# Newton steps of two demodulation weights on GpSimd instead of VectorE, and their squares issued one stage earlier on ScalarE

## The chip, the cores and the metric

The kernel runs on one core of a Trainium2 chip. The metric is the device time of one execution in microseconds, as the median of the runs shown; lower is better. The engines are TensorE (PE: matrix multiplies, PEld: its weight loads), VectorE (DVE), ScalarE (ACT), GpSimd (POOL) and SyncE (SP, which issues the DMA transfers). Each engine executes its own stream of instructions in order and waits on semaphores for the results of the others.

## The reference

The program is a stack of four residual layers over an input of 64 sequences, 64 positions and 256 channels: two attention layers conditioned on a style vector, then two state-space (recurrent) layers. The change touches only the first attention layer, so that is what is shown:

```python
def _dcoef(weight, style):
    return rsqrt(einsum('oi,bi->bo', square(weight), square(style)) + 1e-8)

s1, s2 = styles[:, :256], styles[:, 256:]
x = x * s1[:, None, :]
x = (x - mean(x)) * rsqrt(var(x) + 1e-5)            # over channels
q_dc = _dcoef(q_weight, s1); k_dc = _dcoef(k_weight, s1); v_dc = _dcoef(v_weight, s1)
w_dc = _dcoef(w_weight, s2); u_dc = _dcoef(u_weight, s2)
q = heads((x @ q_weight.T) * q_dc)
k = heads((x @ k_weight.T) * k_dc)
v_flat = (x @ v_weight.T) * v_dc * s2
attn = softmax(q @ k.T * scale)
out  = (attn @ heads(v_flat)) @ w_weight.T * w_dc
skip = v_flat @ u_weight.T * u_dc
return out + skip                                   # added to the layer's input
```

The five vectors `q_dc` to `u_dc`, one value per output channel and sequence, are called demodulation coefficients here. They depend on the weights and the styles only, not on `x`.

## The kernel before

**Layout and staging.** Channels lie on the 128 partitions (two halves of 128), tokens along the free dimension. The 4096 tokens are cut into 8 blocks of 512 for attention; with two layers that makes 16 attention blocks (`Att`, numbered 0 to 15), about 32 us each. After them 16 blocks of the state-space layers follow, driven by a recurrence over time steps. All weights and all of `x` stay on chip.

**The order of the work.** Every instruction is pinned to the program order. The attention part writes this order from a list of events: each part of a block has a due time in units of one block's duration, relative to the block's number (`att_plan`: `(-0.836, "style")` means that block n's `style` is issued at n - 0.836). The events are sorted by due time and called in this order, so an earlier due time only means an earlier place in the stream of each engine; no instruction waits for a clock.

**An attention block.** `style` multiplies `x` by the style, `fold1` adds the two channel halves, `mean` multiplies by a matrix of 1/256 on TensorE (tile `pm`), `center` subtracts that on VectorE and squares on ScalarE (tile `sq`), `fold2` adds the halves of the squares, `var` is the second mean (tile `pv`), `root` takes the logarithm and exponential on ScalarE (tile `rs`), `norm` multiplies. `style`, `fold1`, `fold2` and `norm` run on VectorE for block 0 and on GpSimd for all others (`engine()`). Then come the projections (`q`, `k`, `v`; TensorE tile `pw`), `scores` (tile `ps`, four groups per block), the softmax (`soft_a`: maximum `mx`, subtraction and exponential `pr`; `soft_b`: sum and reciprocal `sm`, then scaling on GpSimd), transposes of the probabilities (`turn`, tile `pt`), transposes of the values (`values`, also named `pv` on the page, shape 64x64 or 128x64; `values_out` copies them on ScalarE into `v`), `attend` (tile `po`), and the two output projections `out` with weights 4 (`u`) and 3 (`w`), whose results are multiplied by the coefficients on VectorE (tile `t`). Small matmul results share three rotating PSUM buffers (`aps`), so a matmul may have to wait for whoever reads the buffer three uses earlier.

**The coefficients.** `demodulate` is a generator that is advanced by events, one stage at each call, for the weights in the order 0, 1, 2, 4, 3 (q, k, v, u, w). Each weight has four stages: (1) the square of the weights on ScalarE (tile `wsq`); (2) eight matmul records on TensorE with the squared styles (tile `dca`) and a copy with bias on ScalarE (tile `newton`); (3) logarithm and exponential on ScalarE (tile `dc`), a first value of the reciprocal root; (4) a Newton step that refines it: two multiplies, one multiply-add and one multiply of 128x128 elements. Stage 4 is on VectorE for the first attention layer and on GpSimd for the second. `first` is the generator of the first layer; the second layer's is advanced later, one stage at a time. The coefficients of weight 4 are first read by block 0's `out` at 0.183 and those of weight 3 by its `out` at 1.422.

At 0.05 four stages of `first` are due at once, all of weight 4; at 0.7 four more, all of weight 3. Around them stand, of block 0: `scores` 0 (-0.243), `soft_a` 0 (-0.054), `v` 1 (-0.050), `scores` 1 (0.034), `soft_a` 1 (0.090), `out` 4 (0.183), `values` 0 (0.213), `values_out` 0 (0.259), `values` 1 (0.341); of block 1: `style` (0.164), `fold1` (0.174), `mean` (0.176), `center` (0.181), `fold2` (0.194), `var` (0.370), `root` (0.386), `norm` (0.402), `q`, `k` (0.522 to 0.693), `v` 0 (0.736); of block 2: `style` (1.164), `fold1` (1.174), `mean` (1.176).

Before block 0, `warm` issues matmuls on constants to keep TensorE busy while the first inputs arrive.

Of the kernel before, what the change touches and what calls it, by code (L numbers as in the profile page):

```python
# [41 lines left out]
def bc(ap, axis, n):  # L42

    ap = ap.unsqueeze(axis)
    shape = list(ap.shape)
    shape[axis] = n
    return ap.broadcast_to(shape)
# [13 lines left out]
def tile_kernel(ctx: ExitStack, tc: tile.TileContext, ins, out):  # L61
    nc = tc.nc
# [43 lines left out]
    def mm(*args, **kw):  # L106
        pin(nc.tensor.matmul(*args, **kw))  # L107
# [4 lines left out]
    def act(*args, **kw):  # L112
        pin(nc.scalar.activation(*args, **kw))  # L113
# [474 lines left out]
    with tc.tile_pool(name="xpool", bufs=1) as xpool, tc.tile_pool(  # L588
# [35 lines left out]
        def demodulate(l, pool, tag):  # L624

            dc = dcs[l] = xpool.tile([P, 5, HC, B], FP, tag=f"dc{l}", name=f"dc{l}")

            kd = kds[l] = xpool.tile([P, HC, B, 2], FP, tag=f"kd{l}", name=f"kd{l}")
            for w in (0, 1, 2, 4, 3):
                wsq = pool.tile([P, HC, H], FP, tag=tag, name=f"wsq{l}_{w}")  # L630
                act(wsq, att_w[l][:, w, :, :], AF.Square)
                yield
                p = aps.tile([P, HC, B], FP, tag="w", name=f"dca{l}_{w}")
                for oc in range(HC):
                    for k in range(HC):
                        mm(
                            p[:, oc, :],
                            wsq[:, k, oc * P : (oc + 1) * P],
                            csq[:, (0 if w < 3 else HC) + k, :],
                            start=(k == 0),  # L640
                            stop=(k == HC - 1),
                        )
                d = dc[:, w, :, :]
                e = a1.tile([P, HC, B], FP, tag="newton", name=f"newton{l}_{w}")
                act(e, p, AF.Identity, bias=eps_dm)
                yield
                act(d, e, AF.Ln)
                act(d, d, AF.Exp, scale=-0.5)
                yield

                eng = nc.vector if l == 0 else nc.gpsimd

                def times(o, a, b):
                    pin(eng.tensor_tensor(o, a, b, ALU.mult))

                times(e, e, d)
                times(e, e, d)

                g = float(H // NH) ** -0.5 if w == 1 else 1.0
                pin(eng.tensor_scalar(e, e, -0.5 * g, 1.5 * g, ALU.mult, ALU.add))  # L660
                times(d, d, e)
                if w == 1:
                    times(d, d, dc[:, 0, :, :])
                    times(kd, bc(d, 3, 2), bc(bc(mask_par, 1, B), 1, HC))
                elif w == 2:

                    times(d, d, cT[:, 2:4, :])
                yield
# [253 lines left out]
        functions()  # L922
        warm(20)
        first, second = demodulate(0, a2, "t4"), demodulate(1, a1, "sq")
        plan0 = prepare(0, lambda name: e8.tile([P, TB], FP, tag="xc", name=name))

# [4 lines left out]
        def at(when, *parts):  # L931
            events.extend((when, b, part, args) for b, part, *args in parts)
# [4 lines left out]

        for when, k in (
            (-0.835, 1), (-0.823, 2), (-0.805, 2), (-0.613, 2), (-0.597, 2), (-0.477, 1),
            (-0.345, 2), (0.05, 4), (0.7, 4),  # L940
        ):
            at(when, *[(first, None)] * k)
        at(-0.822, (warm, None, 14))
# [254 lines left out]
```

## Time and profile before

| | |
|---|---|
| median of 3 runs | 1598.27 us (1596.71 to 1598.61) |
| profiled execution, own time | 1596.88 us |
| its span, first to last instruction | 1595.0 us |
| TensorE busy | 1527.8 us (96%) |
| VectorE busy | 1311.3 us (82%) |
| ScalarE busy | 1121.8 us (70%) |
| GpSimd busy | 862.4 us (54%) |
| mean granted TensorE clock | 0.993 |

A row of the profile names an engine, the line of the program, the operation, and output<-inputs by their tile names without numbers; times are in us. "Idle before, releaser" is how long the engine waited just before the instruction, and which instruction ended that wait. The line can be that of a helper: L107 is every matmul, L110 every transpose, L113 every ScalarE activation, L123 most two-input operations of VectorE, L654 the multiplies of the Newton step and L660 its multiply-add; so the tile names tell the instructions apart. An fp32 matmul appears as two records. "PEclk" is the granted TensorE clock, as a share of full speed, in forty equal slices of the span; TensorE's busy times are modelled and include pipelining.

### The profile page before, as it was taken

Reading aid. Unit: us, or ns where it says so; the run is one execution under the profiler, and the core shown is the slowest. Engines: PE = TensorE matmul, PEld = TensorE weight load, DVE = VectorE, ACT = ScalarE, POOL = GpSimd, SP = SyncE. Lnnn points to the kernel's source line nnn. Section 1 sums busy time; section 2 is a strip of 40 time slices with the busy share of each in tenths; the row PEclk is TensorE's granted clock in tenths of the full one; section 3 lists DMA queues with packets and bytes.
Section 4 is the critical chain, followed back from the end, with each engine's and each line's share of the span. In section 5 each row is a group of like instructions: output and inputs, shape, how many; then the busy total and the mean of one; then the engine's idle time right before and its main releaser. Section 6 shows DMA issues by size and latency. Waiting matters only on the chain. (4 is left out here: it accounts for less than half of the span.)

```text
span 1595.0 us, 30321 instructions
## 1 busy us (share of the span) xinstructions
PE 1527.8 (96%) x12440; PEld 669.0 (42%) x12440; DVE 1311.3 (82%) x1483; ACT 1121.8 (70%) x1899; POOL 862.4 (54%) x859
## 2 busy tenths in 40 slices
PE   8999999999999688999999999999999999999888
PEld 5555555555555333333333333333333333333324
DVE  5776767777777688989999999999899899998776
ACT  3555554455456468888878888887888887887774
POOL 1667566556667657365455464654564545635420
PEclk9999999999999799999999999999999999999999
DMA  7000000000000020000000000000000000000001
GB/s 242 2 1 2 2 2 1 2 2 2 1 2 2 1 64 1 1 1 1 1 1 1 1 1 1 1 1 1 1 8 7 14 1 14 15 1 14 7 8 27
DMA packets 19337, 18.26 MB, mean 11 GB/s; under 512 B 5472, under 2 KB 16352, under 8 KB 19200
## 3 DMA queue, kind: packets, MB, share of 16 engines
q1 hardware_dynamic: 19200, 16.34, 3.2%
q8 instruction: 98, 1.61, 0.4%
q14 instruction: 39, 0.32, 0.1%
HBM read 12.14 MB, written 4.19 MB: 10 GB/s over the span
## 5 line engine op out<-in xcount | busy, mean ns | idle before, releaser
L113 ACT ACTIVATE v<-h,ad 128x512 f32<-128x512 f32 x1008 | 649.0, 711 | 111.2 <-DVE h L1099 109.4
L1099 DVE CUSTOM_DVE_ANT_0 h<-v,pu 128x1024 f32<-128x1024 f32 x504 | 593.7, 1217 | 98.6 <-ACT v L113 50.9
L107 PE MATMUL pu<-xn,bd 32*128 32x512 f32 x2048 | 292.8, 640 | 34.2 <-DVE h L1099 29.8
L107 PE MATMUL py<-h,cd 128*32 128x512 f32 x2048 | 246.3, 598 | 0.0
L206 POOL TENSOR_TENSOR xr<-xr,cT 128x512 f32<-128x512 f32 x55 | 70.5, 1282 | 311.7 <-ACT xr L205 311.6
L107 PE MATMUL pw<-xm,aw 128*128 128x512 f32 x384 | 178.0, 602 | 0.0
L107 PEld LDWEIGHTS pu<-xn,bd 32*128 32x128 f32 x2048 | 82.3, 183 | 172.0 <-issue 99.7
L825 POOL TENSOR_TENSOR pr<-pr,sm 128x1024 f32<-128x1024 f32 x64 | 121.1, 1903 | 21.7 <-DVE sm L824 20.2
L107 PE MATMUL pg<-xt,win 128*128 128x512 f32 x256 | 127.0, 618 | 0.0
L107 PE MATMUL pw<-z,wo 128*128 128x512 f32 x240 | 125.6, 625 | 0.0
L117 DVE SCALAR_TENSOR_TENSOR acc<-xr,cv,acc 128x512 f32<-128x512 f32 x165 | 123.7, 750 | 1.6 <-ACT acc L113 0.2
L107 PE MATMUL acc<-xt,win 128*128 128x512 f32 x256 | 124.3, 609 | 0.7 <-ACT xc L113 0.7
L107 PEld LDWEIGHTS py<-h,cd 128*32 128x32 f32 x2048 | 53.5, 109 | 164.1 <-issue 163.8
L839 ACT COPY pT<-pt 128x512 f32<-128x512 f32 x128 | 68.4, 586 | 76.5 <-PE pt L110 76.5
L113 ACT ACTIVATE pr<-pr 128x1024 f32<-128x1024 f32 x64 | 67.7, 1057 | 60.7 <-DVE pr L123 60.7
L107 PEld LDWEIGHTS pw<-xm,aw 128*128 128x128 f32 x384 | 68.5, 190 | 68.0 <-issue 64.5
L440 POOL TENSOR_TENSOR dx<-xn,rep 128x512 f32<-128x512 f32 x64 | 81.2, 1279 | 18.7 <-DVE ys L123 18.7
L814 DVE TENSOR_REDUCE mx<-ps 128x16 f32<-128x1024 f32 x64 | 78.3, 1224 | 13.7 <-PE ps L107 13.7
L323 POOL TENSOR_TENSOR xn<-xg,rep 128x512 f32<-128x512 f32 x64 | 82.0, 1280 | 8.0 <-ACT xg L113 3.3
L721 POOL TENSOR_TENSOR sq<-sq 128x512 f32<-128x512 f32 x15 | 19.2, 1277 | 122.8 <-ACT sq L113 122.8
L123 DVE TENSOR_TENSOR pr<-ps,mx 128x1024 f32<-128x1024 f32 x64 | 78.4, 1225 | 8.2
L123 DVE TENSOR_TENSOR t<-pw,dc 128x512 f32<-128x512 f32 x64 | 44.2, 690 | 44.9 <-PE pw L107 43.7
(155 smaller groups left out, 2315.0 us busy)
## 6 DMA issues: line engine op xcount, KB each, us to landing
xt<-in_xT SPq DMA_DIRECT2D x8, 512.0 KB, 8.5
out_xT<-xt SPq DMA_DIRECT2D x14, 256.0 KB, 2.3
aw<-in_aw SPq DMA_DIRECT2D x10, 256.0 KB, 6.6
win<-in_win SPq DMA_DIRECT2D x2, 1024.0 KB, 9.0
rep<-in_rep SPq DMA_DIRECT2D x2, 784.0 KB, 7.2
wo<-in_wo SPq DMA_DIRECT2D x2, 512.0 KB, 8.6
out_xT<-xt SPq DMA_DIRECT2D x2, 192.0 KB, 2.5
wx<-in_wx SPq DMA_DIRECT2D x2, 96.0 KB, 7.9
```

What stands on the lines that cost most here:

```text
L107: pin(nc.tensor.matmul(*args, **kw))
L113: pin(nc.scalar.activation(*args, **kw))
L117: nc.vector.scalar_tensor_tensor(out=out, in0=in0, scalar=scalar, in1=in1, op0=op0, op1=op1)
L123: pin(nc.vector.tensor_tensor(*args))
L206: pin(nc.gpsimd.tensor_tensor(curb, curb, bc(temb, 2, BT), ALU.add))
L323: pin(nc.gpsimd.tensor_tensor(self.xn[j], xg, self.rep[:, DI : 2 * DI], ALU.add))
L440: pin(nc.gpsimd.tensor_tensor(self.dx[j], self.xn[j], self.rep[:, 2 * DI : 3 * DI], ALU.mult))
L721: pin(self.engine().tensor_tensor(a, a, self.sq[:, 1, :], ALU.add))
L814: pin(nc.vector.tensor_reduce(mx, s4, AX.X, ALU.max))
L825: pin(nc.gpsimd.tensor_tensor(pr, pr, bc(sm, 3, S), ALU.mult))
L839: pin(nc.scalar.copy(self.pT[g][:, c, :, :], pt))
L1099: nc.vector._custom_dve(TENSOR_ADD_SAT, out=hn, in0=vs.pop((i, h)), in1=pu[h], s0=10.0, s1=-10.0)
```

## The change

The Newton step of weights 4 and 3 of the first attention layer goes from VectorE to GpSimd; for weights 0, 1 and 2 it stays on VectorE. In the event list, one of the four stages due at 0.05 (the square of weight 4) is now due at -0.1, and one of the four due at 0.7 (the square of weight 3) at 0.3. The other three stages of each weight keep their due times.

```diff
@@ in demodulate, stage 4
-                eng = nc.vector if l == 0 else nc.gpsimd
+                eng = nc.vector if l == 0 and w < 3 else nc.gpsimd
@@ the events of the first layer's coefficients
         for when, k in (
             (-0.835, 1), (-0.823, 2), (-0.805, 2), (-0.613, 2), (-0.597, 2), (-0.477, 1),
-            (-0.345, 2), (0.05, 4), (0.7, 4),
+            (-0.345, 2), (-0.1, 1), (0.05, 3), (0.3, 1), (0.7, 3),
         ):
             at(when, *[(first, None)] * k)
```

In the streams of the changed program, GpSimd has the Newton step of weight 4 ahead of block 1's `style` and `fold1`, and that of weight 3 ahead of block 2's. On ScalarE the square of weight 4 stands ahead of the exponential of block 0's first score group, and the square of weight 3 between the two pairs of value copies. The streams of TensorE and SyncE are in the same order as before.

## The prediction

> **What bounds the kernel now.** I read the page first, then the timeline of each engine between 6 and 112 us, where the edited instructions lie, and last the table of granted clocks in the one part of the span where it is low. Columns of a timeline row: start, busy time, engine, line, operation, output<-inputs, shapes, count, and in brackets the idle time before and what ended it.
>
> ```profile
> PE 1527.8 (96%) x12440; PEld 669.0 (42%) x12440; DVE 1311.3 (82%) x1483; ACT 1121.8 (70%) x1899; POOL 862.4 (54%) x859
> PEclk9999999999999799999999999999999999999999
> ```
>
> TensorE is the bound: whatever moves its stream early in the span moves the end. Its gaps in the first 60 us are these (TensorE's timeline):
>
> ```profile
> 31.81 0.70 PE L107 MATMUL ps<-kM,qT 32*64 32x128 f32 x32 [0.73 <-DVE pr L123]
> 33.41 1.10 PE L107 MATMUL dca<-csq,wsq 128*128 128x64 f32 x8 [0.91 <-ACT wsq L113]
> 34.36 1.08 PE L107 MATMUL pm<-fold,ones_h 128*128 128x512 f32 x2
> ...
> 40.42 1.15 PE L107 MATMUL pv<-const,vT 128*64 128x64 f32 x32 [2.19 <-DVE xm L123]
> ...
> 58.29 1.10 PE L107 MATMUL dca<-csq,wsq 128*128 128x64 f32 x8 [1.21 <-ACT wsq L113]
> ```
>
> Two gaps wait for a square on ScalarE (0.91 and 1.21 us). The 2.19 us gap waits for VectorE's centring, which frees the bank of `pm`. VectorE is late there because of the fourth weight (its timeline):
>
> ```profile
> 13.25 1.44 DVE L721 TENSOR_TENSOR sq<-sq 128x512 f32<-128x512 f32 x1 [1.71 <-ACT sq L113]
> ...
> 35.64 0.62 DVE L654 TENSOR_TENSOR newton<-newton,dc 128x128 f32<-128x128 f32 x2 [3.29 <-ACT dc L113]
> 36.29 0.23 DVE L660 TENSOR_SCALAR newton<-newton 128x128 f32<-128x128 f32 x1
> 36.55 0.29 DVE L654 TENSOR_TENSOR dc<-dc,newton 128x128 f32<-128x128 f32 x1
> 36.76 1.22 DVE L814 TENSOR_REDUCE mx<-ps 128x16 f32<-128x1024 f32 x1
> ```
>
> It idles 3.29 us for the exponential and then works 1.20 us (35.64 to 36.84), with the maximum of score group 1 queued behind. GpSimd looks empty meanwhile:
>
> ```profile
> 12.24 1.90 POOL L694 TENSOR_TENSOR xm<-xt,cT 128x1024 f32<-128x1024 f32 x1 [10.76 <-DMA xt<-in_xT]
> 18.75 1.27 POOL L709 TENSOR_TENSOR fold<-xm 128x512 f32<-128x512 f32 x1 [4.61 <-DVE xm L733]
> 41.53 1.27 POOL L721 TENSOR_TENSOR sq<-sq 128x512 f32<-128x512 f32 x1 [21.52 <-ACT sq L113]
> ```
>
> But the first two rows belong to attention block 1, whose `style` has due time 1 - 0.836 = 0.164. They run 20 us early only because GpSimd has nothing before them.
>
> **The change, part by part.** VectorE loses four Newton instructions twice (1.20 us at 35.64, 1.37 us at 60.51); GpSimd gets them. No DMA moves. Their cost on GpSimd is in the rows of the second layer's first weight, same shapes: 93.91 to 95.82, that is 1.91 us:
>
> ```profile
> 93.91 0.99 POOL L654 TENSOR_TENSOR newton<-newton,dc 128x128 f32<-128x128 f32 x2
> 94.99 0.30 POOL L660 TENSOR_SCALAR newton<-newton 128x128 f32<-128x128 f32 x1
> 95.37 0.45 POOL L654 TENSOR_TENSOR dc<-dc,newton 128x128 f32<-128x128 f32 x1
> ```
>
> What matters is the queue. Fourth-weight Newton is due at 0.05, so in GpSimd's stream it now stands ahead of block 1's `style` (0.164) and `fold1` (0.174). In the instruction order of the changed program its first multiply waits for ScalarE and is the first elementwise work on GpSimd. So `style`, `fold1`, and behind them the mean `pm` on TensorE, now wait for an exponential that ends near 34 us.
>
> *Step 1, the start: -0.54.* With `style` gone from 12.24, VectorE's sum of squares at 13.25 no longer shares with it: 1.44 us falls to 0.69 (the row of `fold` at 8.41, same shape, GpSimd idle). TensorE waited 0.54 us for it at 14.84; the warming matmuls before it end at 14.30, so 0.54 is all there is. `root`, `norm` and the projections follow; score groups 0 and 1 start at 27.93 and 31.27.
>
> *Step 2, the fourth square: -0.98.* It is issued at -0.1, ahead of the exponential of group 0, and its 0.61 us fills ScalarE's idle 4.34 us before 31.79. Its `dca` follows the scores without a gap: 31.27 + 0.62 = 31.89, against 33.41.
>
> *Step 3, the new wait.* `dca` to its bias row 1.04 us and to the exponential's end another 1.05 (90.05, 91.09 and 92.14 of the second layer): 33.98. GpSimd wakes after 0.07 (ACT's square ends 41.46, GpSimd starts 41.53), works 1.91, then `style` and `fold1` take 3.25 together (57.57 to 60.82, block 2), and TensorE starts 0.09 later: 33.98 + 0.07 + 1.91 + 3.25 + 0.09 = 39.30. `pm` was at 34.36: **4.94 us later**. All behind it on TensorE waits. VectorE, which finished group 1 by 34.7, waits for `pm` too. From there the stream runs without a gap: 0.96 to `pw`, 1.81 to the first `pv`, 1.08 to the second: 43.15 against 40.42, or +2.73. The old wait of 2.19 is gone, since centring ends at 39.30 + 1.16 + 1.21 = 41.67. What follows is in time: GpSimd's sum of squares ends near 44.1, for a matmul at 46.05; its first softmax scaling near 46.2, for a transpose at 47.6. Steps 1 to 3 come to **+2.73** together.
>
> *Step 4, the clock.* TensorE is now idle from 32.9 to 39.3, 6.4 us; the longest gap there was 2.19, at clock 1.00. What such a gap costs, the trace shows at 532 us (timeline, then clock table: stretch, length, busy times and counts by engine, clock, DMA share, GB/s):
>
> ```profile
> 536.18 1.11 PE L110 MATMUL ptr<-const,xc 128*128 128x128 f32 x4 [4.15 <-ACT pt L282]
> 537.09 3.62 PE L107 MATMUL acc<-xt,win 128*128 128x512 f32 x4
> ```
> ```profile
> 536.00:540.00 4.00, 3.82 (x8) 2.15 (x9) 2.60 (x4) 2.78 (x5) 2.28 (x3) 0.50 0.02 4
> ```
>
> After 4.15 us of idling the clock was 0.50, and four records took 3.62 us that take 1.88 at 518.05. Quarter-microsecond stretches show the low clock from 534.2 to 541.0. From 536.18 to the next group at 541.28 passed 5.10 us, for work that takes 2.88 at full clock (0.53 + 1.82 + 0.53): 2.2 us lost. The Trainium skill ("TensorE: Matmul & The Clock Gate", "What's actually happening") says the clock halves after an idle window of about 3.4 us and returns after a busy one; its 3.4 us at half speed would lose 1.7. The windows run free: in the trace the clock came back 3.4 us after it fell (575.2 to 578.6) but also 13.6 (547.9 to 561.4). Bounds: with half of a window sufficing to raise it, the slow stretch after restart is at least 1.7 us, costing 0.8; at most it is one missed window part plus a full one, some 5.5 us, costing 2.6. I take **2.2**, the row in which TensorE likewise resumed at an already halved clock; by the rule the sum below would be 0.5 smaller.
>
> *Step 5, the fifth weight: -1.47.* Its square moves to 0.3, between the two pairs of value copies on ScalarE; 0.63 us, and the logarithm behind them has its matmul only at 47.1, after copies that end at 46.2. So it is hidden. At 58.29 the wait vanishes. The second block does the same work without that wait: from its projections at 86.51 to those after `dca` at 90.89 is 4.38 us, against 5.85 for block 1 (53.38 to 59.23). Newton stands ahead of block 2's `style` here too: `dca` + 2.09 + 0.07 + 1.91 + 3.25 + 0.09 = 7.41, but `pm` comes 9.08 after `dca` (90.05 to 99.13), so 1.67 us of slack covers it. Without that slack its excess would fall on TensorE.
>
> Sum: +2.73 + 2.2 - 1.47 = **+3.5 us**. The profiled execution took 1596.88 (span 1595.0 and 1.9 around it), so it would take 1600.3; the median shown is 1598.27, 1.4 above it, which gives **1601.7**. Nothing later absorbs it: after 58 us attention is back-to-back matmuls, and the recurrence starts from its end.
>
> **Rivals.** *The clock is not the price* (0.17): if it returned almost at once, +2.73 - 1.47 = +1.3, 1599.5, within the 0.2% (3.2 us) that a measurement of this kernel can tell from no change. For it: gaps of 2.2 at 38 us and 1.7 at 46 us left the clock at 1.00. Against: 6.4 us is longer than the 4.15 that halved it, and at 547.9 a gap of 2.22 was enough.
>
> *The fifth weight gains nothing* (0.20): +2.73 + 2.2 = +4.9, 1603.2, if Newton's place ahead of `style` again delays `pm` by the 1.47. That needs GpSimd 3.1 us slower than the rows say; its instructions there touch one shared tile after another, and VectorE is busy beside them.
>
> *Faster* (0.08): if `style` and `fold1` of block 1 still finished before Newton, GpSimd's 21.52 us of idle would be the room it seems. Then `dca` is at 32.43, group 1's maximum no longer waits (35.2 us instead of 39.2 at its centring), the second `pv` starts near 37.2, and the gain is 3.2 + 1.47: 1593.6. It decides as soon as `pm` starts before about 35 us. The instruction order speaks against it: one in-order queue.
>
> **How the numbers follow.** The likeliest case has 0.55; its own range, with 0.8 to 2.6 for the clock, is 1600.3 to 1602.1 and crosses the 0.2% line at 1601.5, so I split it 0.38 slower and 0.17 same. With the rivals: slower 0.38 + 0.20 = 0.58, same 0.17 + 0.17 = 0.34, faster 0.08. The range goes from 1599.5 less 1.0 (half the spread of the three runs) to 1603.2 with 0.4 more for the clock and 0.9 of that spread: 1598.5 to 1604.5.
>
> **What would show it.** In the changed profile: `pm` of block 1 near 39.3 with a gap of 6.4 us behind GpSimd's `fold`; GpSimd's first elementwise row a Newton multiply near 34; clock 0.5 around 39 to 43 us and `pw` there near 3.5 instead of 1.88; sum of squares on VectorE 0.69; the second `dca` without a wait. A `pm` before 35 would make it wrong, as would a span that has not grown with the gap present.

## The result, and the profile after

The changed kernel takes 1599.47 us (median of 21 runs, 1598.21 to 1601.21), the kernel before 1597.42 us (21 runs, 1596.11 to 1600.55): 2.05 us more. The ratio is 1.0014, 95% interval 1.0008 to 1.0019, which is 1.3 to 3.0 us. So it is slower, but by less than the 0.2% (3.2 us) that the prediction took as the line between slower and same, and by less than the 3.5 us of its sum. The profiled execution took 1599.44 us with a span of 1597.6 us.

GpSimd's timeline of the kernel after (start, busy time, engine, line, operation, output<-inputs, shapes, count, idle time before and its releaser) has the queue that the prediction drew up. The Newton step comes first and waits for ScalarE; `style` and `fold1` of block 1 are pushed from 12 and 19 us to 35 and 37:

```profile
33.40 0.98 POOL L654 TENSOR_TENSOR newton<-newton,dc 128x128 f32<-128x128 f32 x2 [31.92 <-ACT dc L113]
34.47 0.30 POOL L660 TENSOR_SCALAR newton<-newton 128x128 f32<-128x128 f32 x1
34.85 0.45 POOL L654 TENSOR_TENSOR dc<-dc,newton 128x128 f32<-128x128 f32 x1
35.26 1.90 POOL L694 TENSOR_TENSOR xm<-xt,cT 128x1024 f32<-128x1024 f32 x1
37.24 1.26 POOL L709 TENSOR_TENSOR fold<-xm 128x512 f32<-128x512 f32 x1
```

TensorE's timeline shows what that does to the mean `pm`, and that the old gaps before the two `dca` and before the second `pv` are gone:

```profile
30.50 0.70 PE L107 MATMUL ps<-kM,qT 32*64 32x128 f32 x32 [0.73 <-DVE pr L123]
31.13 1.10 PE L107 MATMUL dca<-csq,wsq 128*128 128x64 f32 x8
38.56 2.08 PE L107 MATMUL pm<-fold,ones_h 128*128 128x512 f32 x2 [6.32 <-POOL fold L709]
40.42 3.07 PE L107 MATMUL pw<-vT,aw 128*128 128x512 f32 x4
43.42 2.08 PE L107 MATMUL pv<-const,vT 128*64 128x64 f32 x64
...
60.85 1.00 PE L107 MATMUL dca<-csq,wsq 128*128 128x64 f32 x8
```

`pw` takes 3.07 us where it took 1.88. The clock table (stretch, length, busy times and counts by engine, clock, DMA share, GB/s) has the reason; in finer stretches the low clock lasts from 36.0 to 42.8 us:

```profile
36.00:40.00 4.00, 1.44 (x2) 0.84 (x3) 0.00 (x0) 0.00 (x0) 2.42 (x2) 0.50 0.02 4
```

And VectorE's sum of squares, without GpSimd beside it, has fallen from 1.44 to 0.69 us:

```profile
12.69 0.69 DVE L721 TENSOR_TENSOR sq<-sq 128x512 f32<-128x512 f32 x1 [1.71 <-ACT sq L113]
```

One thing must be taken out before two traces are compared by their clocks. VectorE's very first row waits for the first block of `x`, and it starts at 7.15 us in the trace shown of before, at 6.59 us here, and between 6.24 and 6.94 us in all the others below. In the tables below all times are counted from that row.

### The profile page after: what moved, and what is told of

The parts are those of the page before. It is cut to its first block, busy times and chain, and to the rows that moved or that the text cites. A ratio compares the mean times of both kernels' runs of the same rounds, so it can differ in the third digit from the quotient of the medians.

```text
span 1597.6 us, 30321 instructions
## 1 busy us (share of the span) xinstructions
PE 1529.5 (96%) x12440; PEld 669.8 (42%) x12440; DVE 1307.9 (82%) x1475; ACT 1122.0 (70%) x1899; POOL 865.6 (54%) x867
## 5 line engine op out<-in xcount | busy, mean ns | idle before, releaser
L110 PE MATMUL pt<-const,pr 128*128 128x128 f32 x512 | 70.9, 281 | 9.8 <-ACT pT L839 7.0
```

Source lines behind the costliest of these rows:

```text
L110: pin(nc.tensor.transpose(*args))
```

## The experiments

**One part of the change alone: the engine.** The squares keep their old due times.

```diff
-                eng = nc.vector if l == 0 else nc.gpsimd
+                eng = nc.vector if l == 0 and w < 3 else nc.gpsimd
             (-0.345, 2), (0.05, 4), (0.7, 4),
```

> Only the engine of the two Newton steps changes; the squares stay at 0.05 and 0.7. Theory (GpSimd's queue delays block 1's style and fold, hence its mean): TensorE waits for both squares as before, so `dca` of weight 4 comes about 0.97 us later than with the whole change, `pm` near 40 us with a gap of some 6.3 us before it, clock 0.50 there, and the second gap of 1.21 us at the other `dca` stays: about +2.6 + 1.0 + 1.9 = +5.4 us against the kernel before, ratio near 1.0034. Rival (the loss comes from the earlier squares, which push ScalarE's softmax and value copies): no loss, ratio 1.000 or below.

Measured: 1603.16 us (5 runs), ratio 1.0037 (1.0025 to 1.0050), 5.3 us above before by the medians. TensorE's timeline has both waits for the squares (0.91 before the first `dca`, 1.20 before the second) and the new gap:

```profile
32.20 1.10 PE L107 MATMUL dca<-csq,wsq 128*128 128x64 f32 x8 [0.91 <-ACT wsq L113]
39.64 2.08 PE L107 MATMUL pm<-fold,ones_h 128*128 128x512 f32 x2 [6.34 <-POOL fold L709]
41.50 3.49 PE L107 MATMUL pw<-vT,aw 128*128 128x512 f32 x4
```

The loss belongs to the engine half of the change. Without the earlier squares it would have shown at more than twice the size.

**The other part alone: the squares.** Due times as in the change, both Newton steps on VectorE.

```diff
-            (-0.345, 2), (0.05, 4), (0.7, 4),
+            (-0.345, 2), (-0.1, 1), (0.05, 3), (0.3, 1), (0.7, 3),
                 eng = nc.vector if l == 0 else nc.gpsimd
```

> Only the two squares are issued earlier; both Newton steps stay on VectorE, and block 1's style and fold run early on GpSimd as before. Theory: the first `dca` follows its scores at once (-0.98 us), of which about 1.1 reaches the second `pv`; the second `dca` loses its wait (-1.47): about -2.6 us, ratio near 0.9984, no gap over 2 us on TensorE and clock 1.00 throughout the first 60 us. Rival (the squares displace other work on ScalarE): 1.000 or above.

Measured: 1595.85 us (13 runs), ratio 0.9991 (0.9983 to 0.9999). Faster, as the theory said, by 2.0 us on the medians and some 1.4 on the ratio where it had 2.6; the interval, 0.2 to 2.7 us, just holds that. But the clock was not 1.00. The expectation missed two things. The second Newton step on VectorE now falls beside GpSimd's `fold1` of block 2 (59.64 to 60.90): its two multiplies take 1.93 us where they took 0.78, and TensorE waits further on. First VectorE's timeline, then TensorE's:

```profile
59.12 1.93 DVE L654 TENSOR_TENSOR newton<-newton,dc 128x128 f32<-128x128 f32 x2 [2.41 <-ACT dc L113]
```
```profile
38.81 1.15 PE L107 MATMUL pv<-const,vT 128*64 128x64 f32 x32 [2.19 <-DVE xm L123]
39.89 3.57 PE L107 MATMUL pw<-vT,aw 128*128 128x512 f32 x4
...
44.36 0.69 PE L107 MATMUL ps<-kM,qT 32*64 32x128 f32 x32
...
59.71 0.69 PE L107 MATMUL ps<-kM,qT 32*64 32x128 f32 x32
...
64.78 0.70 PE L107 MATMUL ps<-kM,qT 32*64 32x128 f32 x32 [0.51 <-DVE pr L123]
```

From 59.71 to 64.78 are 5.07 us; before took 4.15 (61.09 to 65.24). That gives back 0.9 us. The other surprise is the `pw` of 3.57 us behind a gap of only 2.19: the low clock came there too (the clock table has 0.69 for this stretch), in a place where the trace of before did not have it. More executions of the kernel before, further down, follow it up.

```profile
39.00:42.00 3.00, 3.00 (x35) 1.79 (x33) 2.93 (x5) 3.00 (x6) 2.08 (x2) 0.69 0.00 0
```

**The whole change, with the Newton step behind `style` and `fold1`.** Only its place in the queue differs from the change.

```diff
-            (-0.345, 2), (-0.1, 1), (0.05, 3), (0.3, 1), (0.7, 3),
+            (-0.345, 2), (-0.1, 1), (0.05, 2), (0.179, 1), (0.3, 1), (0.7, 3),
```

> The whole change, but the Newton step of weight 4 is issued at 0.179 instead of 0.05, that is behind block 1's style and fold in GpSimd's queue and still ahead of the output projection that reads it. Theory (the place in the queue is the price, not the engine): `pm` follows `dca` without a gap near 33.4 us, the second `pv` starts near 37.2 instead of 40.4, and the second gap is gone: about -3.2 - 1.5 = -4.7 us against the kernel before, ratio near 0.9971. Rival (Newton on the slower GpSimd is the price wherever it stands): still slower than before, 1.001.

Measured: 1592.80 us (8 runs, 1592.40 to 1593.25), ratio 0.9970 (0.9960 to 0.9981). It is faster than both kernels. GpSimd's timeline has the same Newton instructions at the same price, but now behind work that was ready, and TensorE runs from `dca` to the third score group without a gap:

```profile
11.88 1.90 POOL L694 TENSOR_TENSOR xm<-xt,cT 128x1024 f32<-128x1024 f32 x1 [10.40 <-DMA aw<-in_aw]
18.39 1.26 POOL L709 TENSOR_TENSOR fold<-xm 128x512 f32<-128x512 f32 x1 [4.61 <-DVE xm L733]
34.34 0.99 POOL L654 TENSOR_TENSOR newton<-newton,dc 128x128 f32<-128x128 f32 x2 [14.69 <-ACT dc L113]
```
```profile
32.07 1.10 PE L107 MATMUL dca<-csq,wsq 128*128 128x64 f32 x8
33.02 1.08 PE L107 MATMUL pm<-fold,ones_h 128*128 128x512 f32 x2
33.93 1.88 PE L107 MATMUL pw<-vT,aw 128*128 128x512 f32 x4
35.74 2.08 PE L107 MATMUL pv<-const,vT 128*64 128x64 f32 x64
```

The slower engine costs TensorE nothing here. This kernel and the change differ only in the place of one Newton step in the queue, and that is 6.7 us by their medians (7.1 when each is counted from the kernel before that was timed beside it).

**The whole change, with the gap filled.** 24 matmuls on constants (48 records) stand between `dca` and `pm`; what they compute is not used.

```diff
         at(-0.612, (warm, None, 10))
+        at(0.06, (warm, None, 24))
```

> The whole change, with 24 matmuls on constants issued behind the first `dca`, which fill TensorE's 6.3 us gap before `pm` for about 5.7 us; their result is not used. Theory (the gap halves the clock, at 1.5 to 2.2 us): clock 1.00 at 36 to 43 us, `pm` at the same place, `pw` behind it 1.9 us for four records instead of 3.07; about 1.9 us faster than the whole change, so +0.2 us against the kernel before, ratio near 1.0001. Rival (the clock costs nothing, the wait alone is the loss): as the whole change, ratio 1.0014.

Measured: 1597.40 us (13 runs), ratio 0.9997 (0.9989 to 1.0005): 2.1 us below the change by the medians (2.5 when each is counted from the kernel before beside it). `pm` still waits for `fold`, but what follows runs at full clock (TensorE's timeline, then a row of the clock table):

```profile
31.71 5.58 PE L107 MATMUL warm<-ones_h 128*128 128x128 f32 x48
38.20 1.12 PE L107 MATMUL pm<-fold,ones_h 128*128 128x512 f32 x2 [0.92 <-POOL fold L709]
39.16 1.88 PE L107 MATMUL pw<-vT,aw 128*128 128x512 f32 x4
...
45.76 0.69 PE L107 MATMUL ps<-kM,qT 32*64 32x128 f32 x32
```
```profile
39.00:42.00 3.00, 3.00 (x39) 1.60 (x39) 2.14 (x3) 1.06 (x1) 0.24 (x1) 1.00 0.00 0
```

From `pm` to the third score group are 7.56 us, in the profiled execution of the change 9.65: the low clock cost it 2.09 us there, and the times of the two kernels agree with that.

**The kernel before, profiled four more times.** No edit; what the expectations call a look is one profiled execution.

> The kernel before, unchanged, profiled in another execution. Theory (the clock is judged over free-running stretches of 3.4 us, so TensorE's 2.19 us gap at 38 us halves it in some executions and not in others, and the profiled execution shown was one without): about half of such looks show clock 0.50 for 3.4 us or more behind that gap, and take about 1.5 us longer from the second `pv` to the third score group (3.85 us at full clock). Rival (only gaps above about 3 us halve it): no look shows it.

> As the first look: by the theory about half of the looks have the low clock behind the 2.19 us gap, by the rival none.

> As the first look: by the theory about half of the looks have the low clock behind the 2.19 us gap, by the rival none.

> As the first look: by the theory about half of the looks have the low clock behind the 2.19 us gap, by the rival none.

Measured (times of these executions: 1598.75, 1597.92, 1596.86, 1596.33 us): one of the four has the low clock behind the 2.19 us gap and pays for it. TensorE's timeline of the first, and its clock behind the gap:

```profile
39.96 1.15 PE L107 MATMUL pv<-const,vT 128*64 128x64 f32 x32 [2.19 <-DVE xm L123]
41.04 3.46 PE L107 MATMUL pw<-vT,aw 128*128 128x512 f32 x4
44.30 1.28 PE L107 MATMUL pv<-sq,ones_h 128*128 128x512 f32 x2
45.51 0.69 PE L107 MATMUL ps<-kM,qT 32*64 32x128 f32 x32
```
```profile
42.00:45.00 3.00, 3.00 (x5) 1.09 (x4) 1.71 (x3) 1.31 (x3) 3.00 (x3) 0.53 0.00 0
```

From the second `pv` to the third score group it takes 5.55 us instead of 3.85: 1.70 lost. In the second and third the clock is at 0.50 around 35 us, behind the small gaps of 0.73 and 0.91 us. It costs nothing there, because the slow matmuls only fill the wait for VectorE (timeline of the second):

```profile
34.11 2.00 PE L107 MATMUL pm<-fold,ones_h 128*128 128x512 f32 x2
35.90 2.70 PE L107 MATMUL pw<-vT,aw 128*128 128x512 f32 x4
38.53 1.15 PE L107 MATMUL pv<-const,vT 128*64 128x64 f32 x32
40.19 1.15 PE L107 MATMUL pv<-const,vT 128*64 128x64 f32 x32 [0.51 <-DVE xm L123]
```

The fourth has no low clock there. So with the execution shown ahead of the change it is 1 in 5 that pays behind this gap. That it happens in some executions and not in others is as the theory said. Its share of a half is not refuted by five, and the rival, which expected none, falls.

**The changed kernel, profiled two more times.** No edit.

> The changed kernel, unchanged, profiled in another execution. Theory (the 6.3 us gap always holds one free-running stretch without work, but the clock returns only at the end of a busy one): `pm` about 32 us after VectorE's first row, the clock 0.50 when TensorE resumes in every look, and from `pm` to the third score group between 8.5 and 10.3 us, where full clock would take 7.6 (warmed gap) and the look shown took 9.65. Rival (the low clock is a matter of chance here too): a look at clock 1.00 with 7.6 us.

> As the first look: by the theory clock 0.50 at the restart and 8.5 to 10.3 us from `pm` to the third score group; by the rival a look at full clock and 7.6 us.

Measured (1598.69 and 1598.89 us): `pm` stands 31.98 and 31.97 us after VectorE's first row, the clock is 0.50 at the restart in both, and from `pm` to the third score group are 9.22 and 9.41 us. TensorE's timeline of the first:

```profile
38.51 2.08 PE L107 MATMUL pm<-fold,ones_h 128*128 128x512 f32 x2 [6.34 <-POOL fold L709]
40.37 2.64 PE L107 MATMUL pw<-vT,aw 128*128 128x512 f32 x4
...
47.73 0.69 PE L107 MATMUL ps<-kM,qT 32*64 32x128 f32 x32
```

With the execution shown, three of three pay: 2.09, 1.66 and 1.85 us over the 7.56 of the filled gap, mean 1.87. What each pays is about half of the time that the clock stays low after `pm` starts: it comes back at 42.8, 41.9 and 42.3 us, that is after 4.2, 3.4 and 3.8 us. With the engine changed alone it comes back at 44.8, after 5.2 us, and the price is 10.07 less 7.56, or 2.51.

Counted from VectorE's first row, in us ("group" is the third score group of block 0, "block 1" the first score group of block 1, "end" the end of the span):

| kernel | profiled executions | `pm` | group | block 1 | end | measured against before, medians |
|---|---|---|---|---|---|---|
| before, shown | 1 | 27.21 | 37.12 | 53.94 | 1587.9 | |
| before, all | 5 | 26.45 to 27.21 | 36.36 to 38.76 | 53.18 to 55.58, mean 54.11 | 1587.7 to 1590.2, mean 1588.7 | |
| after | 3 | 31.97 to 31.98 | 41.20 to 41.62 | 56.55 to 56.97, mean 56.75 | 1590.2 to 1591.0, mean 1590.6 | +2.05 |
| engine only | 1 | 32.96 | 43.03 | 59.86 | 1594.0 | +5.28 |
| squares only | 1 | 26.19 | 37.81 | 53.16 | 1589.0 | -2.03 |
| behind `fold1` | 1 | 26.32 | 33.83 | 49.17 | 1584.7 | -5.08 |
| gap filled | 1 | 31.96 | 39.52 | 54.87 | 1590.3 | -0.48 |

What follows block 1 is not the same in every execution: from there to the end the five of before take between 1533.7 and 1535.4 us. Up to about 500 us their distances stay as they were at block 1. They change between 530 and 590 us, where the clock falls to 0.50 three times in each, at places of the work that differ (first from 534.2 to 541.0 in the trace shown, from 535.9 to 539.3 in the second of the four). In the trace shown and the fourth they fall alike, and these two also take alike, 1533.9 and 1533.7 us. That the clock is what changes the distances fits this, but was not tested. One profiled execution is therefore good for the place of a loss, and only to within a microsecond or two for the whole; those of the squares alone, of the kernel behind `fold1` and of the filled gap were also each the slowest run of their kernel.

## Why the prediction was right, and what was mis-sized

The direction, the place and the mechanism hold: the Newton step on GpSimd stands ahead of work that was ready, a 6.3 us gap opens before `pm`, and the gap brings the low clock. The time of 1599.47 us lies inside the range, but 2.2 us below the 1601.7 of the likeliest case. Of that, 0.85 us is the kernel before itself (1598.27 us in the three runs ahead of the change, 1597.42 in the 21 beside it), and 1.4 is the change: the kernel lost 2.05 us, not 3.5. So terms of the sum were too large, and the outcome fell on the other side of the 0.2% line from what was held likeliest. It lies on the 1599.5 that the first rival named; that is a coincidence, since its mechanism is refuted below.

- *Step 1, the start (-0.54).* Mis-sized: -0.75. Counted from the first row, score group 1 starts at 23.91 us in the kernel after and at 24.66 in the trace of before. The floor that I set, the modelled end of the warming matmuls, is none: `pv` starts at 13.58 while their modelled busy time runs to 13.74. The whole 0.75 us of slowed VectorE work came back. TensorE's timeline of the kernel after:

```profile
10.40 3.34 PE L107 MATMUL warm<-ones_h 128*128 128x128 f32 x28
13.58 1.05 PE L107 MATMUL pv<-sq,ones_h 128*128 128x512 f32 x2
```

- *Step 2, the fourth square (-0.98).* Right: `dca` follows its scores by 0.63 us in the kernel after.
- *Step 3, the wait (+2.73 with steps 1 and 2).* The delay of `pm` is 4.76 us (31.97 against 27.21) where I had 4.94; the difference is about what step 1 was too small by. At full clock, which the filled gap shows, the third score group is 2.40 us later than in the trace of before (39.52 against 37.12).
- *Step 4, the clock (2.2).* It is 1.87 us in the mean of three executions. The row at 536 us was a fair stand-in, but its slow stretch behind the restart was longer, 4.8 us (536.2 to 541.0) against 3.4 to 4.2; the 1.7 estimated from the Trainium skill's rule ("TensorE: Matmul & The Clock Gate", "What's actually happening") was a little nearer.
- *Step 5, the fifth weight (-1.47).* Right to the hundredth: from the third score group to block 1's first are 15.35 us in all three executions of the kernel after and 16.82 in before. The slack covered the second Newton step.

With these terms the sum is +2.40 + 1.87 - 1.47 = +2.80 against the one trace of before.

- *The base of the sum* is the term that I did not have. That "gaps of 2.2 at 38 us and 1.7 at 46 us left the clock at 1.00" was true of the execution shown and not of the kernel: one in five pays 1.70 us there, and another started its way through the first 25 us 0.76 us earlier, since its second block of `x` came later and GpSimd's `style` missed VectorE's sum of squares (12.51 us, 0.69 long). Over five executions before stands at 54.11 and after at 56.75: +2.64.
- *"Nothing later absorbs it"* was too strong. At the end of the span the means are 1588.7 and 1590.6, or +1.9, beside the measured 2.05. The executions of before take 0.7 us longer than those of after behind block 1 in the mean, though the one shown (1533.9 us) does not. With spreads of 1 to 2 us in so few executions this is an account of the size and no proof of it.

Of the rivals, the faster one names what would have to be otherwise, and making it so gave what it said: from the traces 3.2 us at the second `pv` and 4.77 at block 1, where 3.2 and 4.7 were predicted; the times give 5.1 by the medians, 3.0 to 6.4 by the interval. The rival that the clock is not the price falls with the filled gap, where `pm` waits as long and the time is 2.1 us shorter. The rival that the fifth weight gains nothing falls with step 5.

The moved squares gained less with the Newton steps on VectorE than they do in the change: 0.9 us is lost again beside GpSimd. So moving the second Newton step was worth something once its square comes early, and moving the first one only in the right place.

## What to carry to other kernels

An idle engine with an in-order queue is not free room: what counts is what stands behind the moved instruction in that queue, and which of it was ready long before. Put the instruction that waits longest behind the ones that are ready, which here was one due time and 6.7 us. And when a price depends on a chance of the single execution, as the clock does here, one profile is not the base of the sum: take several.

## What the runs showed of the hardware that I had not expected

The low clock does not need a long gap. It came behind a gap of 2.19 us in one execution of before and in that of the squares alone, and behind gaps of 0.73 and 0.91 us close together in two more. In the trace of before the changes of the clock around 550 us lie at multiples of about 3.4 us (534.2, 541.0, 547.9, 561.4, 575.2, 578.6), so it seems to be judged over free-running stretches of that length, of which a part without work can be enough; how large a part was not measured. The Trainium skill (the same page, "HAM oscillation — how this bites in real kernels") warns of gaps above some 3.4 us; these runs show it below that. A hint in the same direction, and no more, is that the kernel with the Newton step behind `fold1`, which has no such gap, has the narrowest times: 0.85 us between the slowest and fastest of 8 runs, against 4.3 us in 28 runs of before. More runs spread further by themselves, and the filled gap has 2.4 us in 13.

VectorE's multiplies and adds with both inputs in SBUF all but stand still beside GpSimd: 0.69 us became 1.39 to 1.54 (sum of squares, beside `style`), and a pair of 0.61 us became 1.57 to 2.34 (Newton, beside `style` or `fold1`). In the third extra execution of before (GpSimd's timeline, then VectorE's) the pair runs from 13.11 to 15.45 us while `style` runs from 13.08 to 14.98:

```profile
13.08 1.90 POOL L694 TENSOR_TENSOR xm<-xt,cT 128x1024 f32<-128x1024 f32 x1 [11.60 <-DMA xt<-in_xT]
```
```profile
13.11 2.34 DVE L654 TENSOR_TENSOR newton<-newton,dc 128x128 f32<-128x128 f32 x2
```

"GPSIMD Engine Reference" of the Trainium skill ("Specifications") states that the two engines contend for SBUF when a VectorE instruction has two inputs there. These traces agree, and show that the wait can be most of the GpSimd instruction; it is why GpSimd work that is moved away can pay on VectorE.
